# A four-layer graph kernel: the last layer norm is taken out of the head of the last stage and spread over the end of the stage before it

## The chip, the cores and the metric

The kernel runs on one NeuronCore of a Trainium2 chip. Its engines are called here as the profile calls them: PE multiplies matrices (PEld is its weight load, which the profile lists apart), DVE is the vector engine, ACT the scalar engine, POOL the third elementwise engine, and SP issues the transfers from HBM. Each engine works through its own instructions in order, and they wait for each other through semaphores. The metric is the device time of one execution in microseconds (us); lower is better.

## The reference

There are N = 3327 nodes with D = 64 features each, and a dense 0/1 adjacency matrix of 3327 x 3327 (about 0.5% ones). Four layers follow each other. Each one takes a layer norm without weights, a ReLU, a graph layer, and adds the outcome to x:

```python
def _layernorm(x, axis=-1, eps=1e-5):
    m = jnp.mean(x, axis=axis, keepdims=True)
    v = jnp.var(x, axis=axis, keepdims=True)
    return (x - m) / jnp.sqrt(v + eps)
...
    h = jnp.maximum(_layernorm(x, axis=-1), 0.0)
    x = x + _L2_gnn_ref(h, adj, adj, ...)      # layer 2: two GRU cells and an attention term
    h = jnp.maximum(_layernorm(x, axis=-1), 0.0)
    x = x + _L3_gnn_ref(h, adj, r, w_att, b_att)   # layer 3: hyperbolic graph layer
```

Layers 0 and 3 are hyperbolic layers: a sigmoid of pairwise scores, masked by the adjacency and weighted by a function of the pairwise inner products. Layer 1 is a sum with halving weights. Layer 2 is a GRU cell on the sum over neighbours, and a second GRU cell on the mean over neighbours. The change stands where layer 2 ends and layer 3 begins. Layer 3 needs from each row of x its mean, its variance, and the sum of squares of the positive part of the centred row.

## The kernel before

**Layout.** The nodes are padded to 26 tiles of 128 rows (T = 26, P = 128, NP = 3328). `X` holds x in SBUF as 128 partitions x 26 tiles x 64 columns, fp32. Two tiles, t and t + 13, make a pair, so that a turned (transposed) form has 128 rows: 64 features of the one, 64 of the other. `HP` = 1664 is the width of that form. Adjacency masks stay in SBUF as fp8 from layer 1 on.

**Stages.** `hyperbolic_series(None, ...)` is layer 0; it calls `plain_decay` (layer 1), which calls `plain_gat` (layer 2); a second call, `hyperbolic_series(r3, ...)`, is layer 3. A hyperbolic series has a head (layer norm, factors for each node, fp16 parts, turned operands), a long loop over 4 column chunks x 26 row blocks (matmuls at L643/L644, sigmoid L629, mask product L632, arctangent L649, product L654, sums L664/L672), and a tail that puts the result together and stores it.

**The end of layer 2.** In `plain_gat` the columns of the turned form are cut into four groups, `COLS = (0, 4), (4, 3), (7, 3), (10, 3)` (first tile, number of tiles). The eight steps `u` (two GRU cells x four groups) run as a pipeline: products on PE (L1987, L1992), sigmoids (L2000) and tanh (L2011) on ACT, the rest on DVE (L2007, L2008, L2020 to L2027). The result of a group is a sum of up to four fp32 tiles (`oP`, `xh[0][0]`, `hP`, `deg`), still turned. `turn_back(k)` turns it back on PE: for each tile of the group, one matmul for each term of the sum, with the term as the stationary operand and the 128 x 128 identity as the moving one, added up in PSUM (L2043). The last group has one term and uses a transpose (L2041). `scale(k)` then multiplies by the node's diagonal entry `dcol`, on ACT tile by tile (L2059), for the last group on DVE in one go (L2054), and `use(k)` adds to `X` on DVE (L2063).

**Banks and slots.** PSUM is held as four slots of two banks each; `banks` lists them in the order `cnt[0], cnt[1], acc[0], acc[1]`, two entries for each slot, so entries 4 and 5 are one slot, 6 and 7 another. Waits between engines are set by slot, not by bank. The four groups go into entries 4 to 7. `products(u)` uses entries 4 to 7 for even `u` and 0 to 3 for odd `u`.

**The head of layer 3.** All of it is written in one order for all engines (`manual_schedule`), and so is the end of layer 2. On DVE: row means of X in two halves (L449, L450), centring into `H` (L452), variance from squares that ACT makes (L453, L458, L459), an inverse root by bit tricks (L128 to L142, `root_by_bits`), the sum of squares of the positive part (ACT: L455, L456; DVE: L466, L469), then small factors (L471 to L479), the scaled rows `Xr` (L481), the fp16 parts (ACT L482, DVE L484). PE turns those (L542, L517), ACT and DVE copy them out (L524, L522), and the loop begins at L643. POOL fills constant parts of `X0` and `Xe` (L436, L437, L439) and makes a few fp16 columns of each node's factors (L493 to L506), which PE needs from the second half of the turning on. SP fetches the first four `late` tiles for a count that the loop makes (L1447); these reuse memory of layer 2.

**The tail.** When the sums are done, DVE makes the factors `ah`, `am`; ACT multiplies the first 22 tiles of `M` by `am` (L923) while DVE scales `Xr` and adds it and then `M` to X (L916, L919), and X is stored.

Of the kernel before, what the change touches and what calls it, by code (L numbers as in the profile page):

```python
# [10 lines left out]
F32 = mybir.dt.float32  # L11
# [10 lines left out]
P = 128  # L22
# [27 lines left out]
def tile_gnn4(ctx: ExitStack, tc: tile.TileContext, x, adjT, att0, b0, w1, bias1, w_gat, a_gat,  # L50
# [299 lines left out]
    def hyperbolic_series(r, params, ok, masks=None, done=None, ahead=None, then=None, checks=None):  # L350
# [15 lines left out]
        KE = D + 9  # L366
        left_row = rows[0 if r is None else 1]
        W = 512
        with ExitStack() as st:
# [60 lines left out]
            with room(name="hsp", bufs=1) as tp, room(name="hsps", bufs=2, space=PSUM) as ps, \  # L430
                    tc.manual_schedule(engines={mybir.EngineType.Activation, mybir.EngineType.DVE,
                                                mybir.EngineType.PE, mybir.EngineType.Pool}):
                H, R, sq, sr = [tp.tile([P, T, D], F32, name=n) for n in ("H", "R", "sq", "sr")]
# [13 lines left out]
                mean, v, rv, ax, ia2 = [new(n) for n in ("mean", "v", "rv", "ax", "ia2")]  # L447
                for ts in HALVES:
                    V.reduce_sum(mean[:, ts], X[:, ts, :], axis=AX.X)  # L449
                V.tensor_scalar(mean, mean, 1.0 / D, None, op0=OP.mult)  # L450
                for ts in HALVES:
                    V.tensor_sub(H[:, ts, :], X[:, ts, :], wide(mean[:, ts]))  # L452
                    A.activation(sq[:, ts, :], H[:, ts, :], AF.Square)  # L453
                for ts in HALVES:
                    A.activation(R[:, ts, :], H[:, ts, :], AF.Relu)  # L455
                    A.activation(sr[:, ts, :], R[:, ts, :], AF.Square)  # L456
                for ts in HALVES:
                    V.reduce_sum(v[:, ts], sq[:, ts, :], axis=AX.X)  # L458
                V.tensor_scalar(v, v, 1.0 / D, LN_EPS, op0=OP.mult, op1=OP.add)  # L459
                sd, q1, q2 = new("sd"), new("q1"), new("q2")  # L460
                steps = root_by_bits(sd, q1, q2, v)
                next(steps)
                V.reciprocal(rv, v)
                for _ in range(3):
                    next(steps)
                V.reduce_sum(x2[:, HALVES[0]], sr[:, HALVES[0], :], axis=AX.X)  # L466
                for _ in steps:
                    pass
                V.reduce_sum(x2[:, HALVES[1]], sr[:, HALVES[1], :], axis=AX.X)  # L469
                if r is not None:  # L470
                    V.tensor_scalar(rv, rv, cc, None, op0=OP.mult)  # L471
                V.tensor_mul(x2, x2, rv)
# [95 lines left out]
                V.tensor_scalar(right, right, bcol, None, op0=OP.add)  # L568
# [343 lines left out]
            with room(name="hse", bufs=1) as tp:  # L912
# [9 lines left out]
                for t in range(own.start):  # L922
                    A.activation(M[:, t, :], M[:, t, :], AF.Copy, scale=am[:, t:t + 1])  # L923
# [1277 lines left out]
```

## Time and profile before

| what | value |
|---|---|
| median of 3 runs | 721.82 us (719.4 to 724.04) |
| profiled execution, its own time | 719.45 us |
| span of that execution in the profile | 717.7 us |
| busy share PE / DVE / ACT / POOL | 89% / 74% / 76% / 60% |
| end of layer 2 after the last GRU product, 447.4 to 461.3 us | PE busy 9.1 of 13.9 us, DVE 8.5, ACT 6.1 |
| head of layer 3 up to the first `Xr`, 461.3 to 472.7 us | PE idle, DVE busy 10.8 of 11.4 us, ACT 5.2 |
| rest of the head, 472.7 to 488.7 us | PE 13.1 of 16.0 us, DVE 14.1, ACT 10.9, POOL 10.4 |
| loop of layer 3, 488.7 to 693 us | PE busy 203.1 of 204.3 us |

Times inside the execution count from the start of the span. The profile's timeline gives, for each row, start, duration, engine, line, operation, the tile written and the tiles read, and in brackets the idle time before it and whom it waited for; rows of the same kind are merged ("x8"). The chain of waits follows the execution back from its last instruction: each piece is what the next one waited for. Granted clock is the share of full speed that PE had. A matmul in fp32 appears as two records, each with its own weight load.

### The profile page before, as it was taken

How to read it: one execution, taken by the hardware profiler on the slowest of the kernel's cores; microseconds unless marked ns; L12 is line 12 of the kernel's file. 1: busy time of each engine (PE TensorE's matmuls, PEld its weight loads, DVE VectorE, ACT ScalarE, POOL GpSimd, SP SyncE). 2: the span in 40 equal slices, each digit the busy share in tenths (PEclk: the TensorE clock that was granted, in tenths of full speed). 3: DMA queues.
4: the chain of work that ended last, by engine and by line, in shares of the span. 5: the costliest groups of instructions: out<-in, count | busy, mean ns of one | idle time of the engine just before them, and what ended most of it. 6: DMA issues, size and time to landing. Idle time of an engine off the chain costs nothing.

```text
span 717.7 us, 12120 instructions
## 1 busy us (share of the span) xinstructions
PE 636.2 (89%) x4291; PEld 261.4 (36%) x4291; DVE 532.8 (74%) x990; ACT 542.1 (76%) x718; POOL 433.4 (60%) x329
## 2 busy tenths in 40 slices
PE   0799999999999889989998999459999999999970
PEld 0522233333333333435445653443223433333320
DVE  5967778777777799999755428697776877778756
ACT  3688888888888695687881479359888888888853
POOL 2799999989999400205730000039888788887840
PEclk9999999999999999999999999969999999999995
DMA  3998888898878716489960000203325345443001
GB/s 64 313 301 274 259 268 266 277 288 273 268 245 271 258 69 215 137 291 333 402 243 1 2 1 1 95 18 96 89 82 147 105 120 146 116 119 115 25 1 52
DMA packets 61638, 119.25 MB, mean 166 GB/s; under 512 B 9568, under 2 KB 34048, under 8 KB 61568
## 3 DMA queue, kind: packets, MB, share of 16 engines
q1 hardware_dynamic: 57216, 118.38, 51.2%
q10 hardware_dynamic: 4352, 0.02, 0.3%
q8 instruction: 35, 0.57, 0.3%
q14 instruction: 35, 0.29, 0.1%
HBM read 115.64 MB, written 0.88 MB: 162 GB/s over the span
## 4 chain that ended last, share of the span: by engine, by line
PE 67%; DVE 12%; issue 6%; POOL 6%; ACT 4%; DMA 3%; ACTq 1%; POOLq 0%; DVEq 0%
PE slot L664 17%; PE slot L672 9%; PE slot L643 9%; PE slot L1564 9%; PE slot L644 8%; POOL sig L632 6%; PE slot L1578 5%; PE slot L1871 5%; DMA adj<-in 3%; PE slot L1987 2%; PE slot L2043 1%; PE slot L1992 1%; DVE X L1617 1%; ACTq L322 1%; ACT sig L629 1%
## 5 line engine op out<-in xcount | busy, mean ns | idle before, releaser
L654 DVE SCALAR_TENSOR_TENSOR sig<-slot,sig 128x768 f32<-128x768 f32 (+2 forms) x209 | 212.8, 1018 | 105.6 <-POOL sig L632 104.2
L649 ACT ACTIVATE slot<-slot 128x768 f32<-128x768 f32 (+1 forms) x208 | 177.2, 852 | 53.3 <-PE slot L644 53.1
L632 POOL TENSOR_TENSOR sig<-adj,sig 128x768 f32<-128x768 f32 (+2 forms) x105 | 201.7, 1943 | 12.9 <-ACT sig L629 8.4
L629 ACT ACTIVATE sig<-leftB,right 128x768 f32<-128x768 f32 (+2 forms) x210 | 203.5, 970 | 0.5 <-PE pt L517 0.5
L632 POOL TENSOR_TENSOR sig<-mask,sig 128x768 f32<-128x768 fp8e4 (+3 forms) x106 | 173.6, 1651 | 38.2 <-ACT sig L629 37.3
L664 PE MATMUL slot<-sig,Xr 128*64 128x384 f32 (+1 forms) x832 | 169.9, 526 | 3.7 <-DVE sig L654 3.4
L643 PE MATMUL slot<-XC,XT 128*128 128x384 f16 (+1 forms) x416 | 142.2, 342 | 3.1 <-ACT sum L682 1.7
L644 PE MATMUL slot<-XF,XE 73*128 73x384 f16 (+1 forms) x416 | 141.6, 340 | 0.0
L672 PE MATMUL slot<-sig,X 128*32 128x384 f32 (+1 forms) x832 | 94.2, 525 | 0.0
L1570 ACT ACTIVATE w<-slot,ebias 128x832 bf16<-128x832 f32 x76 | 69.0, 951 | 25.3 <-PE slot L1564 24.9
L664 PEld LDWEIGHTS slot<-sig,Xr 128*64 128x64 f32 x832 | 49.8, 135 | 85.7 <-issue 62.7
L643 PEld LDWEIGHTS <-XT 128*128 128x128 f16 x416 | 40.6, 98 | 93.8 <-issue 67.4
L1564 PE MATMUL slot<-mask,rest 128*128 128x416 fp8e4 x208 | 53.9, 341 | 5.0 <-ACT adj L1570 2.8
L1564 PE MATMUL slot<-mask,after 128*128 128x416 fp8e4 x208 | 53.4, 339 | 1.3 <-DVE deg L1588 1.3
L644 PEld LDWEIGHTS <-XE 73*128 73x128 f16 x416 | 40.8, 98 | 28.6 <-issue 4.0
L1459 DVE TENSOR_SCALAR_CACHE_REDUCE same<-late 128x832 fp8e4<-128x832 f32 x48 | 48.4, 1009 | 0.0
L219 POOL TENSOR_TENSOR mask<-mask,offdiag 128x128 fp8e4<-128x128 fp8e4 x26 | 17.5, 684 | 44.4 <-PE slot L1564 44.3
L436 POOL MEMSET X<- 128x832 f32 x2 | 1.6, 791 | 69.6 <-ACT xh L1978 69.6
L1871 PE MATMUL slot<-mask,own 128*64 128x384 fp8e4 (+1 forms) x416 | 39.6, 345 | 2.6 <-DVE deg L1588 2.6
L672 PEld LDWEIGHTS slot<-sig,X 128*32 128x32 f32 x832 | 16.4, 108 | 67.7 <-issue 67.7
L542 PE MATMUL pt<-ident_h,Xp 128*64 128x128 f16 x32 | 2.6, 314 | 37.7 <-ACT Xp L482 37.7
L1578 PE MATMUL slot<-w,h 128*64 128x416 bf16 x304 | 34.0, 345 | 0.0
(341 smaller groups left out, 696.2 us busy)
## 6 DMA issues: line engine op xcount, KB each, us to landing
adj<-in SPq DMA_DIRECT2D x78, 384.0 KB, 5.2
late<-in SPq DMA_DIRECT2D x48, 416.0 KB, 3.2
adj<-in SPq DMA_DIRECT2D x17, 832.0 KB, 7.2
adj<-in SPq DMA_DIRECT2D x27, 512.0 KB, 5.8
ahead<-in SPq DMA_DIRECT2D x14, 832.0 KB, 7.7
ahead<-in SPq DMA_DIRECT2D x16, 416.0 KB, 5.7
own<-in SPq DMA_DIRECT2D x16, 416.0 KB, 5.8
own<-in SPq DMA_DIRECT2D x8, 832.0 KB, 10.1
```

Of the source, the lines that this page charges most:

```text
L629: A.activation(sig[:, os], leftB[c][:, os], AF.Sigmoid, bias=right[:, b:b + 1])
L632: G.tensor_tensor(sig[:, os], adj[:, os], sig[:, os], op=OP.mult)
L643: PE.matmul(L[:, o, :c[1] * P], XT[:, rows], XC[c][:, o, :], start=True, stop=False)
L644: PE.matmul(L[:, o, :c[1] * P], XE[:KE, rows], XF[c][:, o, :], start=False, stop=True)
L649: A.activation(L, L, AF.Arctan, scale=PA / SX ** 2)
L654: V.scalar_tensor_tensor(sig[:, os], slot[:, os, :tiles[k][0][1] * P], PC, sig[:, os], op0=OP.add, op1=OP.mult)
L664: PE.matmul(acc[c][o * D:(o + 1) * D, 0, :n], Xr[:, b, :], sigs[k][:, o, :], start=b == 0, stop=b == T - 1)
L672: PE.matmul(acc[c][q:q + 32, 1, :n], X0[:, b - 1 + i, :], w[:, o, :], start=b == 1, stop=b == T - 1, tile_position=(0, q))
L1564: PE.matmul(cnt[o][:, h, :BK], w, cols(k, o, h), start=w is after and steps[k][1] == T - 1, stop=True, skip_group_check=True)
L1570: A.activation(ws[k][:, o, :, :], cnt[o][:, :, :BK], AF.Exp, scale=-LN2, bias=ebias)
L1578: PE.matmul(acc[c][o * D:(o + 1) * D, h, :BK], parts[i][:, b, :], w[:, o, h, :], start=b == T - 1 and i == 0, stop=b == 0 and i == 1)
L1871: PE.matmul(acc[k][o * D:(o + 1) * D, :], w, mask[:, of(k, o * HP)], start=n == 0 and i == 0, stop=n == T - 1 and i == 1)
```

## The change

The second layer norm is prepared inside layer 2.

- In block 12 of layer 2's loop, `centre()` takes the row means of X (kept in `ln.mean`) and subtracts them from X in place.
- Every tile of the GRU result is turned back with `centring` (identity minus the mean over each half of 64) in place of the identity, so that what is added to X has mean zero and X stays centred. The last group becomes a matmul like the others.
- The mean of what was added is needed too, since x itself needs it at the end. `turn_means()` repeats all products with a 128 x 2 moving operand `means` into PSUM entry 7. `new_means()` adds the result to `ln.mean`.
- The four groups go to entries 4, 6, 0 and 2, one in each slot.
- Group 1 is scaled and added on DVE, tile by tile (`use_at_once`), not by ACT and DVE.
- Squares, positive parts, their squares and the row sums are made group by group behind each addition, in tiles of the GRU that are free by then (`xh`). Variance, root, `x2` and the reciprocal are finished there.
- Layer 3 takes `H = X`, and its own means, centring, squares and sums are left out. The mean comes back as the bias of an ACT instruction: for 22 tiles in the tail, for the last 4 in the head.

```diff
                                                 mybir.EngineType.PE, mybir.EngineType.Pool}):
-                H, R, sq, sr = [tp.tile([P, T, D], F32, name=n) for n in ("H", "R", "sq", "sr")]
+                H = R = sq = sr = None
+                if ln is None:
+                    H, R, sq, sr = [tp.tile([P, T, D], F32, name=n) for n in ("H", "R", "sq", "sr")]
                 Xe = tp.tile([P, T, KE + 9], F16, name="Xe")
                 E, Fe = Xe[:, :, D:KE], Xe[:, :, KE:]
                 G.memset(X0, 0.0)
...
-                mean, v, rv, ax, ia2 = [new(n) for n in ("mean", "v", "rv", "ax", "ia2")]
...
+                ax, ia2, q1, q2 = [new(n) for n in ("ax", "ia2", "q1", "q2")]
+                x2s = x2 if ln is None else ln.x2
+                if ln is None:
...
+                else:
+                    H, rv, sd = X, ln.rv, ln.sd
                 if r is not None:
                     V.tensor_scalar(rv, rv, cc, None, op0=OP.mult)
-                V.tensor_mul(x2, x2, rv)
+                V.tensor_mul(x2, x2s, rv)
                 V.tensor_scalar(ax, x2, 1.0, None, op0=OP.subtract)
                 V.reciprocal(ia, ax)
                 V.tensor_scalar(root, x2, 1.0, None, op0=OP.max)
...
                     copy_on(on, XF[c][:, o, :], turned16(lambda t: Xp[:, t, D:], KE, *range(t, t + c[1])))
                 V.tensor_mul(right, lr[:, :, 1], z)
                 V.tensor_scalar(right, right, bcol, None, op0=OP.add)
+                if ln is not None:
+                    for t in range(own.start, own.stop):
+                        A.activation(X[:, t, :], X[:, t, :], AF.Identity, bias=ln.mean[:, t:t + 1])
                 V.scalar_tensor_tensor(root, root, ROOT, zs, op0=OP.mult, op1=OP.mult)
                 V.tensor_scalar(small["k"], ia, 0.5 * PF, None, op0=OP.mult)
                 V.tensor_scalar(small["bx"], ax, -1.0, None, op0=OP.mult)
...
                 def added(a, ts):
                     V.tensor_add(X[:, ts, :], X[:, ts, :], a[:, ts, :])
 
-                own = slice(T - 4, T)
                 for t in range(own.start):
-                    A.activation(M[:, t, :], M[:, t, :], AF.Copy, scale=am[:, t:t + 1])
+                    A.activation(M[:, t, :], M[:, t, :], AF.Identity, scale=am[:, t:t + 1], bias=ln.mean[:, t:t + 1])
                 for ts in HALVES:
                     scaled(Xr, ah, ts)
                     added(Xr, ts)
...
             xh = [[pers.tile([P, HP], F32, name=f"xh{g}{o}") for o in range(2)] for g in range(2)]
             oP = H.rearrange("p k o d -> p (k o d)")
             wgT = pers.tile([D, D], F32, name="wgT")
+            centring = pers.tile([P, P], F32, name="centring")
+            means = pers.tile([P, 2], F32, name="means")
+            G.memset(means, 0.0)
+            for o in range(2):
+                G.memset(means[o * D:(o + 1) * D, o:o + 1], 1.0 / D)
+            V.tensor_sub(centring.rearrange("p (o d) -> p o d", o=2), ident.rearrange("p (o d) -> p o d", o=2),
+                         wide(means))
             hundred = pers.tile([P, 1], F32, name="hundred")
             V.memset(hundred, -100.0)
             for _ in range(1):
...
                     V.scalar_tensor_tensor(deg, deg, -1.0, r0, op0=OP.mult, op1=OP.mult)
                     V.scalar_tensor_tensor(deg, deg, 2.0, r0, op0=OP.add, op1=OP.mult)
 
-                todo = {3: lambda: degrees(2, 4), 4: lambda: degrees(3, 6), 12: lambda: (weights2(4), inverse()),
+                def centre():
+
+                    V.reduce_sum(ln.mean, X, axis=AX.X)
+                    V.tensor_scalar(ln.mean, ln.mean, 1.0 / D, None, op0=OP.mult)
+                    V.tensor_sub(X, X, wide(ln.mean))
+
+                todo = {3: lambda: degrees(2, 4), 4: lambda: degrees(3, 6), 12: lambda: (weights2(4), inverse(), centre()),
                         13: lambda: turn(0, 6), 15: lambda: weights3(5), 17: inverse2, 19: lambda: turn(4, 7),
                         20: lambda: turn(8, 4), 23: lambda: turn(12, 6)}
                 V.tensor_scalar(zo[:, 2 * T:2 * T + 2], zo[:, 2 * T:2 * T + 2], first, None, op0=OP.mult)
...
                 d2 = dcol.rearrange("p (h t) -> p h t", h=2)
                 turned, scaled = {}, {}
 
+                BACK = 4, 6, 0, 2
+
+                def terms_of(k):
+                    return [oP] if k == C - 1 else [oP, hP, deg] if k > 1 else [oP, xh[0][0], hP, deg]
+
                 def turn_back(k):
 
-                    terms = [oP] if k == C - 1 else [oP, hP, deg] if k > 1 else [oP, xh[0][0], hP, deg]
                     t0, n = COLS[k]
-                    pt = turned[k] = bank(4 + k)
+                    pt = turned[k] = bank(BACK[k])
                     for t in range(n):
-                        cs = slice((t0 + t) * P, (t0 + t + 1) * P)
-                        for i, src in enumerate(terms):
-                            if len(terms) == 1:
-                                PE.transpose(pt[:, t * P:(t + 1) * P], src[:, cs], ident)
-                            else:
-                                PE.matmul(pt[:, t * P:(t + 1) * P], src[:, cs], ident, start=i == 0,
-                                          stop=i == len(terms) - 1)
+                        product(pt[:, t * P:(t + 1) * P], k, t0 + t, centring)
+
+                def product(to, k, t, w):
+                    terms = terms_of(k)
+                    for i, src in enumerate(terms):
+                        PE.matmul(to, src[:, t * P:(t + 1) * P], w, start=i == 0, stop=i == len(terms) - 1)
+
+                def turn_means():
+                    pt = turned["means"] = bank(7)[:, :2 * C2]
+                    for k in range(C):
+                        for t in range(COLS[k][0], COLS[k][0] + COLS[k][1]):
+                            product(pt[:, 2 * t:2 * t + 2], k, t, means)
+
+                def new_means():
+                    t = tp.tile([P, 2, C2], F32, name="dm")
+                    V.tensor_mul(t, turned["means"].rearrange("p (t h) -> p h t", h=2), d2)
+                    V.tensor_add(halves(ln.mean), halves(ln.mean), t)
+
+                def halves(t):
+                    return t.rearrange("p (h t) -> p h t", h=2)
 
                 def of_bank(k):
                     n = COLS[k][1]
...
                 def use(k):
                     t0, n = COLS[k]
                     V.tensor_add(X2[:, :, t0:t0 + n, :], X2[:, :, t0:t0 + n, :], scaled[k][:, :, :n, :])
+
+                def use_at_once(k):
+                    t0, n = COLS[k]
+                    for h in range(2):
+                        for t in range(n):
+                            to = X2[:, h, t0 + t, :]
+                            V.scalar_tensor_tensor(to, of_bank(k)[:, h, t, :], d2[:, h, t0 + t:t0 + t + 1], to,
+                                                   op0=OP.mult, op1=OP.add)
+
+                sq, pos, sr = xh[1][0], xh[1][1], xh[0][1]
+
+                def group(t, k):
+                    t0, n = COLS[k]
+                    return t.rearrange("p (h t d) -> p h t d", h=2, d=D)[:, :, t0:t0 + n, :]
+
+                def squares(k):
+                    t0, n = COLS[k]
+                    A.activation(group(sq, k), X2[:, :, t0:t0 + n, :], AF.Square)
+
+                def positive(k):
+                    t0, n = COLS[k]
+                    A.activation(group(pos, k), X2[:, :, t0:t0 + n, :], AF.Relu)
+
+                def squares_of_positive(k):
+                    A.activation(group(sr, k), group(pos, k), AF.Square)
+
+                def variance(k):
+                    t0, n = COLS[k]
+                    V.reduce_sum(halves(ln.v)[:, :, t0:t0 + n], group(sq, k), axis=AX.X)
+
+                def norms2(t0, n):
+                    V.reduce_sum(halves(ln.x2)[:, :, t0:t0 + n],
+                                 sr.rearrange("p (h t d) -> p h t d", h=2, d=D)[:, :, t0:t0 + n, :], axis=AX.X)
 
                 for k in (2, 3):
                     mean(k)
...
                 tanh(K - 1)
                 scale(0)
                 turn_back(1)
-                scale(1)
                 turn_back(2)
                 state(K - 1)
+                turn_back(3)
+                turn_means()
                 use(0)
-                turn_back(3)
-                use(1)
+                squares(0)
+                positive(0)
+                use_at_once(1)
+                squares(1)
+                variance(0)
+                variance(1)
                 scale(2)
                 scale(3)
+                use(3)
+                squares(3)
                 use(2)
-                use(3)
+                squares(2)
+                for k in (0, 1, 3, 2):
+                    if k:
+                        positive(k)
+                    squares_of_positive(k)
+                variance(3)
+                variance(2)
+                V.tensor_scalar(ln.v, ln.v, 1.0 / D, LN_EPS, op0=OP.mult, op1=OP.add)
+                steps = root_by_bits(ln.sd, *ln.qs, ln.v)
+                next(steps)
+                V.reciprocal(ln.rv, ln.v)
+                for _ in range(3):
+                    next(steps)
+                norms2(0, COLS[2][0])
+                for _ in steps:
+                    pass
+                norms2(COLS[2][0], C2 - COLS[2][0])
+                new_means()
 
     def load():
         for ts in HALVES:
...
     wt, bias, wg, gru = middle_weights()
     zo = const.tile([P, 2 * T + 2 + EARLY + len(LATE)], F32, name="zo")
     first = const.tile([P, 1], F32, name="first")
+    ln = SimpleNamespace(mean=const.tile([P, T], F32, name="mean2"), qs=[bias[:, i * T:(i + 1) * T] for i in range(2)],
+                         **{n: wt[:, i * T:(i + 1) * T] for i, n in enumerate(("v", "x2", "rv", "sd"))})
     V.memset(first, 0.0)
     for o in (0, D):
         V.memset(first[o:o + 1, :], 1.0)
```

`V` is DVE, `A` ACT, `G` POOL. The hunks left out pass `ln` along as an argument.

## Prediction

> **What bounds the kernel now.** I read the page first, then the chain of waits, then the timeline and the groups of instructions around 447 to 489 us. By stages the change can only act between the last GRU product (447.4 us) and the loop of layer 3 (488.7 us). Before it nothing on the path moves, and behind it the loop keeps PE busy for 203.1 of 204.3 us, so a shift of its start is a shift of the end. The chain there, with start and duration in us:
>
> ```profile
> 447.49 3.78 PE slot L2043 x32
> 451.30 1.75 ACT x L2059 x8
> ...
> 453.10 4.96 PE slot L2043 x42
> 458.05 0.34 PE slot L2041 x3
> ...
> 458.42 1.34 ACT x L2059 x6
> ...
> 460.34 0.95 DVE X L2063 x2
> ...
> 465.49 1.97 DVE v L458 x2
> ...
> 472.72 1.98 DVE Xr L481 x2
> ```
>
> PE turns four groups, the end of that is added to X by 461.29, and 11.4 us of layer norm on DVE follow until `Xr` starts at 472.72. The second group waits, since its bank lies in the slot that ACT still reads:
>
> ```profile
> 451.30 1.74 ACT L2059 ACTIVATE x<-slot,dcol 128x64 f32<-128x64 f32 x8 [0.41 <-PE slot L2043]
> 453.10 0.49 PE L2043 MATMUL slot<-ident,own 128*128 128x128 f32 x2 [1.83 <-ACT x L2059]
> ```
>
> **What the change removes.** With one slot for each group that wait goes. Records of L2043 follow each other every 0.1115 us (42 of them, with 0.1 to open, from 453.10 to the next line's first at 457.89). So 32 + 42 records from 447.42, and 6 for the last group, which is now three products of two records, end at 456.4 instead of 458.4: 2.0 us. The data are there: the last state (L2027) ends at 453.42, before PE reaches its group at 455.7. The means (L449, L450: 2.2 us) and the centring (L452: 2.0, half of it under ACT's squares) go from the head. In block 12 they cost 2.0 + 0.2 + 1.9 us on DVE between 401.0 and 410.8, where DVE waits 9.7 us for ACT's L1937. Without that cover it would be 4.1 us.
>
> **What it adds: `turn_means`.** The four groups have 4 x 4 + 3 x 4 + 3 x 3 + 3 x 1 = 40 products, repeated with two moving columns. The stationary operand is still a whole 128 x 128 fp32 tile, loaded anew for each of two records: 80 weight loads. Nothing in the trace has just this form, so its price is bounded from rows.
>
> ```profile
> L664 PEld LDWEIGHTS slot<-sig,Xr 128*64 128x64 f32 x832 | 49.8, 135 | 85.7 <-issue 62.7 <-DVE sig L654 22.6 <-DVE same L1459 0.2
> L672 PEld LDWEIGHTS slot<-sig,X 128*32 128x32 f32 x832 | 16.4, 108 | 67.7 <-issue 67.7
> L2043 PEld LDWEIGHTS slot<-ident,deg 128*128 128x128 f32 x20 | 3.0, 192 | 0.0
> ```
>
> The mean of one fp32 load goes 108, 135, 192 ns for 32, 64, 128 columns: 0.87 ns a column over a fixed 80 ns, so 0.11 us of streaming for 128. The starts say the same. Two loads that open a burst overlap only in the fixed part:
>
> ```profile
> 447.42 0.30 PEld L2043 LDWEIGHTS slot<-ident,own 128*128 128x128 f32 x2 [0.60 <-ACT gate L2000]
> 478.90 1.24 PEld L560 LDWEIGHTS <-XT 128*128 128x128 f16 x26
> ```
>
> 0.30 less 0.19 is a start every 0.11 us for fp32. The fp16 loads of L560, with six moving columns, come about every 0.03 us ((1.24 - 0.10) / 25 is 0.046 with one pause in it), and that at half clock. [...] by the rows above 80 x 0.108 = 8.7 us. [...] I take 8.7 us at full clock. [...] Above: 80 x 0.192 = 15.4 with nothing overlapped.
>
> Who waits: entry 7 lies in the slot of entry 6, where group 1 is. `turn_means()` is written ahead of `use_at_once(1)`, so that DVE instruction waits for the last mean product, not for group 1 (ready at 453.7). Queued behind it on DVE are both first variance sums, `scale(3)` and `use(3)`, `use(2)`; on ACT `squares(1)` waits for it, with `scale(2)` and all later squares behind. So the norm's work starts over at T, the end of `turn_means`: 456.4 + 8.7 = 465.1 at full clock. Only `use(0)`, `squares(0)`, `positive(0)` lie under it.
>
> **The clock.** [...] The window rows list stretch, length, busy time of PE, PEld, DVE, ACT and POOL with counts, granted clock, DMA:
>
> ```profile
> 381.04:384.45 3.41, 1.53 (x15) 1.08 (x15) 1.79 (x4) 0.00 (x0) 0.00 (x0) 1.00 0.02 5
> 384.45:387.86 3.41, 3.41 (x19) 2.15 (x20) 1.28 (x2) 0.00 (x0) 0.00 (x0) 0.50 0.00 0
> 459.55:462.96 3.41, 0.00 (x0) 0.00 (x0) 3.14 (x5) 0.20 (x1) 0.00 (x0) 1.00 0.97 370
> 462.96:474.70 11.74, 0.00 (x0) 0.00 (x0) 11.14 (x27) 6.06 (x7) 2.50 (x5) 0.50 0.07 28
> ```
>
> A stretch of 3.41 us with PE 45% busy was enough to halve the clock for the next one, and so was one with no matmul. In `turn_means` PE has weight loads without a gap, but two moving columns per 0.108 us. [...] whether loads alone count as busy, no row here shows. If they don't, the drop falls at the end of the first stretch that is less than half dense: between 458.1 and 461.5, about 459.8. Then 31 of 80 records are done and 49 follow at 2 x 0.107: T = 470.4 (468.7 to 472.2). If they count, T stays 465.1.
>
> **From T to `Xr`.** DVE: six tiles at the 0.196 us spacing of L1617's 128 x 64 form plus latency, 1.3. ACT then: squares(1) 0.5 and scale(2) 1.3, to T + 3.2. DVE meanwhile: sums of groups 0 and 1 (0.6 + 0.5), scale(3) 0.5, use(3) 0.6, then use(2), to T + 4.0. ACT: squares(2) 0.5, then 0.6 and three times 1.0 for the positive parts and their squares, to T + 8.1. DVE: last norm sum 0.95, then x2, ax, reciprocal, two factors as at L472 to L479, 1.4: `Xr` at T + 10.4. (ACT durations from L453's 0.89 for 832 columns and L2000's 0.87 ns a column.) That is one us shorter than the 11.4 behind 461.29; splitting into groups takes back most of what left the path. The DVE chain of root steps lies under ACT here.
>
> Small ones. POOL's fill of `X0` and `Xe` (0.8 + 0.7) now waits for the last norm sum, since those tiles reuse what it reads. The fp16 columns then are ready 7.2 us after `Xr` starts, not 6.0; PE asks for them at 7.35: 0 to 0.5, I take 0. The `late` fetches wait for mean products, so they start near T instead of 457.9, the fourth at T + 9; the first of them is counted at 489.6 + shift, and chunk operands queued behind on SP (479.2) are later too: 0. Four ACT additions of the mean (0.9) fit in ACT's 1.8 us wait before `leftB`. The tail's ACT has a bias more at 0.244 spacing: 0 to 0.3, I take 0. PE stays idle past the next stretches either way, so the head's start at half clock (until 480.02) remains. None of these can fall below nothing: they only move or add work.
>
> **Sum and rivals.** `Xr` starts at T + 10.4 against 472.72.
> - *Clock drops under the mean products*, chance 0.66: 470.4 + 10.4 - 472.7 = +8.1 us (+6.4 to +9.9). On the profile's own 719.45 that is 727.6; on the median of 721.82, which lies 2.4 higher, 729.9. For it: the 45% row. Against it: gapless loads.
> - *Clock holds*, 0.26: +2.8, 724.6. Slower still, within what can be told.
> - *Mean products are cheap* (not slower), 0.08: loads at L560's pace end at 458.5 to 458.7, so T + 10.4 = 469.1, -3.7 us, 718.1. It decides below 0.071 us a record, where T is 462.3. Against it stand the 0.11 us starts of every fp32 burst. The change then would do what it says: group work under PE.
>
> A measurement of this kernel tells about 1%, 7.2 us, from no change. Of the first case about three quarters lie beyond it. Hence slower 0.50, within 0.48, faster 0.02. The range 723.3 to 732.3 holds the first two cases with the spread of medians (1.5) on the first's late drop; it leaves out the third and the tails. The first case's own is 727.5 to 732.3.
>
> **What would show it.** In the profile after: group records without the 1.8 us wait, ending near 456.4; 80 mean records with starts 0.108 apart, then 0.21 once the clock reads 0.50; the first DVE `X<-slot` tile waiting for PE, not before 465; `Xr` 10.4 us behind the last mean product; loop and tail as long as before. Starts of 0.03 us, or a wait that ends with group 1 near 453.7, would prove me wrong.

## The result and the profile after

The changed kernel takes 731.8 us (median of 4 runs, 731.47 to 733.88) against 721.62 us for the kernel before (median of 4 runs, 719.4 to 724.04). The ratio is 1.0146, with a 95% interval of 1.0109 to 1.0184: slower by 10.2 us. The profiled execution has a span of 729.6 us, 11.9 us more than the profile of before. 1.6 us of that are there when the turning of the groups begins. They are older than the changed parts of layer 2: the first product of layer 0's loop is 1.2 us later (32.07 against 30.91), the first of layer 2's loop 1.7 us (381.80 against 380.14). In all the kernels below the first record of the turned groups lies between 446.4 and 449.7 us, in one of them at 446.85 although nothing ahead of the groups differs from the kernel before. So I count from that record (447.42 us before, 449.04 us after); counted so, the two profiles are 10.3 us apart.

These timeline rows of the changed kernel answer to the rows of the groups shown of before:

```profile
449.04 0.49 PE L2069 MATMUL slot<-centring,own 128*128 128x128 f32 x2
...
457.40 0.83 PE L2069 MATMUL slot<-centring,own 128*128 128x128 f32 x6
458.07 0.28 PE L2069 MATMUL slot<-means,own 128*128 128x2 f32 x2
...
468.76 1.42 PE L2069 MATMUL slot<-means,own 128*128 128x2 f32 x6
470.22 1.05 DVE L2109 SCALAR_TENSOR_TENSOR X<-slot,dcol,X 128x64 f32<-128x64 f32 x5 [14.57 <-PE slot L2069]
```

The groups run without a gap and are through 9.2 us after their first record; before it took 11.0. Then come the 80 mean records, and the first tile of `use_at_once(1)` waits on DVE for 14.57 us until the last of them is done. Its group's last record had ended at 455.56, and DVE has been idle since 455.65.

The windows of the same stretch (length, busy us of PE, PEld, DVE, ACT and POOL with counts, granted clock, DMA share, GB/s) show the clock:

```profile
449.04:458.07 9.03, 9.03 (x84) 9.03 (x81) 6.40 (x13) 4.55 (x13) 0.00 (x0) 1.00 0.01 2
458.07:463.52 5.45, 5.45 (x52) 5.45 (x50) 0.00 (x0) 0.00 (x0) 0.00 (x0) 1.00 0.00 0
463.52:470.22 6.70, 6.66 (x32) 6.57 (x31) 0.00 (x1) 0.00 (x0) 0.00 (x0) 0.50 0.12 16
```

In the first 5.45 us of the mean products 49 of the 80 records go by, 0.1115 us from one start to the next. Then the clock is halved, with PE and its weight loads busy throughout, and the last 31 take 6.7 us, about 0.215 each. DVE and ACT do next to nothing in either row.

Behind that wait, three rows of the timeline are longer than I had them. The end of the norm:

```profile
479.32 0.80 POOL L439 MEMSET X<- 128x832 f32 x1 [97.61 <-DVE dm L2079]
479.37 1.27 DVE L480 TENSOR_SCALAR ax<-x 128x26 f32<-128x26 f32 x1
480.05 0.23 POOL L440 MEMSET Xe<- 128x78 f16 x1
480.15 0.46 POOL L442 MEMSET Xe<- 128x26 f16 x3
481.52 1.97 DVE L488 SCALAR_TENSOR_TENSOR Xr<-X,ia 128x832 f32<-128x832 f32 x2
```

The same step in the kernel before:

```profile
471.59 0.18 DVE L473 TENSOR_SCALAR ax<-x 128x26 f32<-128x26 f32 x1
```

The first sigmoid of layer 3, with PE's last transposes of `Xe` ahead of it, and the sigmoid and its product on POOL in the kernel before:

```profile
492.80 0.94 PE L524 MATMUL pt<-ident_h,Xe 128*82 128x128 f16 x10 [0.19 <-DVE XE L529]
493.82 2.37 ACT L639 ACTIVATE sig<-leftB,right 128x512 f32<-128x512 f32 x3 [1.47 <-DVE XE L529]
494.62 2.16 POOL L642 TENSOR_TENSOR sig<-mask,sig 128x512 f32<-128x512 fp8e4 x2 [6.26 <-ACT sig L639]
```
```profile
483.45 1.32 ACT L629 ACTIVATE sig<-leftB,right 128x512 f32<-128x512 f32 x2
484.24 2.16 POOL L632 TENSOR_TENSOR sig<-mask,sig 128x512 f32<-128x512 fp8e4 x2 [4.76 <-ACT sig L629]
```

Before, the sigmoid ran as soon as ACT had made `leftB`; now it is 1.47 us behind that. The row names DVE's copy as what ended the wait, but the sigmoid starts 0.08 us behind the end of PE's last transposes (493.74).

And the scaling of `M` at the end, here and in the kernel before:

```profile
715.59 7.40 ACT L932 ACTIVATE M<-M,mean,am 128x64 f32<-128x64 f32 x22 [5.20 <-DVE am L870]
722.37 1.22 DVE L929 TENSOR_TENSOR X<-X,M 128x448 f32<-128x448 f32 x2 [1.29 <-ACT M L932]
```
```profile
705.36 5.36 ACT L923 ACTIVATE M<-M,am 128x64 f32<-128x64 f32 x22 [5.20 <-DVE am L860]
709.34 2.03 DVE L919 TENSOR_TENSOR X<-X,M 128x832 f32<-128x832 f32 x3
```

With that, the 10.3 us have their places. "Tile" is the start of the first `use_at_once(1)` tile on DVE; all values are in us. The first two columns count from the first group record, the next three are lengths: from `Xr` to the first product on POOL, from there to the scaling of `M`, from there to the end of the span. The last is the span's end, from the first group record.

| kernel | tile | Xr | to POOL | loop | tail | end |
|---|---|---|---|---|---|---|
| before | - | 25.3 | 11.5 | 221.1 | 12.3 | 270.3 |
| after | 21.2 | 32.5 | 13.1 | 221.0 | 14.0 | 280.6 |
| difference | | +7.2 | +1.6 | -0.1 | +1.7 | +10.3 |

### The profile page after: what moved, and what is told of

Same layout as the page of the kernel before. It is cut to its first block, busy times and chain, and to the rows that moved or that the text cites. A ratio compares the mean times of both kernels' runs of the same rounds, so it can differ in the third digit from the quotient of the medians.

```text
span 729.6 us, 12298 instructions
## 1 busy us (share of the span) xinstructions
PE 649.5 (89%) x4374; PEld 275.4 (38%) x4374; DVE 535.8 (73%) x998; ACT 544.6 (75%) x722; POOL 431.4 (59%) x332
## 5 line engine op out<-in xcount | busy, mean ns | idle before, releaser
L642 POOL TENSOR_TENSOR sig<-adj,sig 128x768 f32<-128x768 f32 (+2 forms) x105 | 201.7, 1947 | 14.5 <-ACT sig L639 11.0
L219 POOL TENSOR_TENSOR mask<-mask,offdiag 128x128 fp8e4<-128x128 fp8e4 x26 | 15.3, 598 | 46.8 <-PE slot L1573 46.8
```

The source lines that it names most:

```text
L642: G.tensor_tensor(sig[:, os], adj[:, os], sig[:, os], op=OP.mult)
```

## The experiments

My theory after the prediction and these rows: the mean products cost their weight loads, stretched by a halved clock, and all of it counts because one DVE instruction waits for them; three smaller costs stand behind it. The rival was that the norm by groups is long in itself. Each ratio below is to the kernel before in runs taken together with the experiment's (medians 720.85 to 721.13 us), and the experiments start from the changed kernel, but for the last.

**Without the means.**

```diff
                 turn_back(3)
-                turn_means()
...
-                new_means()
```

> The changed kernel without turn_means and new_means. Left out: the mean of what the GRU adds is not added to the mean of X. Times here are counted from the first record of the group products (before: Xr at +25.3 us; after the change: first X<-slot tile at +21.2, Xr at +32.5). Theory 1, the 80 mean records on PE stand ahead of the first X<-slot tile and of everything behind it: that tile starts at about +5.0 to +6.6, when group 1 is turned and the first use is done, and Xr at +16.5 to +18, so 15 us earlier than with the change. With the tail's +2.0 and the first sigmoid's +1.4 still there the kernel is 4 to 5 us faster than before. Rival, the norm by groups is long in itself and the mean products only fill time in which ACT and DVE would have worked anyway: Xr comes 5 us earlier at most (+27 or later), and the kernel stays slower than before by 5 us.

Measured: 0.9932 (0.9911 to 0.9953) of before, 4.9 us faster. The timeline of this kernel:

```profile
452.95 1.24 DVE L2109 SCALAR_TENSOR_TENSOR X<-slot,dcol,X 128x64 f32<-128x64 f32 x6
...
464.66 1.97 DVE L488 SCALAR_TENSOR_TENSOR Xr<-X,ia 128x832 f32<-128x832 f32 x2
```

From the first group record at 446.39 that is +6.6 for the tile and +18.3 for `Xr`, 14.2 us earlier than with the means; `Xr` is 0.3 past the range that I had given. The rival falls. The tile no longer waits, and the norm behind it is about as long as with the means (11.7 us against 11.3).

**The means in another slot.**

```diff
-                    pt = turned["means"] = bank(7)[:, :2 * C2]
+                    pt = turned["means"] = bank(5)[:, :2 * C2]
```

> The changed kernel with the means in entry 5 instead of 7, that is, in the slot of group 0, whose reader is done, and not in that of group 1. The same 80 records. Theory 1, the wait of the first X<-slot tile is for the slot and not for PE's time as such: the tile starts at +5 to +6.6 from the first group record instead of +21.2, the norm runs beside the mean products, and what still waits for their end is new_means, the last DVE step before Xr. Xr then is 1.4 to 2.5 us behind the last mean record (+21.1): +22.5 to +23.6, against +25.3 before and +32.5 with the change. The whole is within 1.5 us of before, with the tail and the first sigmoid still later. Rival, PE's time is what counts, whoever waits: Xr stays near +32.5 and the kernel 10 us slower than before.

Measured: 1.0025 (1.0009 to 1.0041), 1.8 us slower than before, 723.02 us in the median against 731.8 with the change. Its timeline:

```profile
455.17 1.05 DVE L2109 SCALAR_TENSOR_TENSOR X<-slot,dcol,X 128x64 f32<-128x64 f32 x5
...
464.67 0.80 POOL L439 MEMSET X<- 128x832 f32 x1 [83.39 <-DVE wt L2134]
...
470.24 0.18 DVE L2079 TENSOR_TENSOR dm<-slot,dcol 128x26 f32<-128x26 f32 x1 [5.78 <-PE slot L2069]
...
470.56 0.17 DVE L480 TENSOR_SCALAR ax<-x 128x26 f32<-128x26 f32 x1
...
471.62 1.97 DVE L488 SCALAR_TENSOR_TENSOR Xr<-X,ia 128x832 f32<-128x832 f32 x2
```

The total is 0.3 us over what I expected, with an interval of 0.6 to 3.0 us. The same 80 records, ending no earlier than with the change (+21.6 against +21.2), but the tile goes at +6.6 and `Xr` at +23.0. The slot was the wait; one digit moves it from the first step of the norm to the last, `new_means`, which sits 5.78 us idle. The fill of `X0` falls into that idle time, and `ax` takes 0.17 us.

**The mean products with 128 moving columns.**

```diff
-            means = pers.tile([P, 2], F32, name="means")
+            means = pers.tile([P, P], F32, name="means")
...
-                            product(pt[:, 2 * t:2 * t + 2], k, t, means)
+                            product(pt[:, 2 * t:2 * t + P], k, t, means)
```

> The changed kernel with 128 moving columns in each mean product (the two of the means and 126 of zeros, which later products overwrite) instead of two. The same 80 weight loads. Theory 1, a record costs its load, and the clock fell because only two columns moved: records stay 0.1115 us apart to the end, the clock reads 1.00 under all of them, and the last ends at +18.0 from the first group record instead of +21.1; Xr at +29.3, the kernel 3 us less slow than with the change (+7 us on before). Rival A, the clock falls at that point for another reason: 0.50 from +14.5 again and an end at +21 or later. Rival B, the moving columns cost too: records over 0.15 apart at full clock and an end beyond +21.

Measured: 1.0097 (1.0058 to 1.0135), 7.0 us slower than before. The windows of the mean products (columns as above), and the tile:

```profile
457.75:463.50 5.75, 5.75 (x54) 5.75 (x53) 0.00 (x0) 0.00 (x0) 0.00 (x0) 1.00 0.00 0
463.50:466.89 3.39, 3.35 (x31) 3.16 (x29) 0.00 (x0) 0.00 (x0) 0.00 (x0) 1.00 0.00 0
```
```profile
466.89 1.24 DVE L2110 SCALAR_TENSOR_TENSOR X<-slot,dcol,X 128x64 f32<-128x64 f32 x6 [11.54 <-PE slot L2069]
```

Sixty-four times as many moving columns, and the products end 3.0 us sooner (+18.2 against +21.2). So the columns don't set the price: a record takes 0.1115 us at full clock with 2 or with 128 of them, and the weight loads are busy in 5.75 of the first 5.75 us. And the clock read 1.00 through all 80 records, 9.1 us, where the only difference is the columns that move; how many are needed was not tried.

**The means in the same product as the tile.** If a record takes 0.1115 us with 2 or with 128 columns and two more are next to free, the means can be columns 129 and 130 of the centring matrix.

```diff
-            centring = pers.tile([P, P], F32, name="centring")
-            means = pers.tile([P, 2], F32, name="means")
+            both = pers.tile([P, P + 2], F32, name="both")
+            centring, means = both[:, :P], both[:, P:]
...
-                        product(pt[:, t * P:(t + 1) * P], k, t0 + t, centring)
+                        product(last if t == 3 else pt[:, t * BOTH:(t + 1) * BOTH], k, t0 + t, both)
```

`BOTH` is 130. Four such tiles, 520 columns, don't fit into the 512 of an entry, so the fourth tile of group 0, `last`, lies in entry 5.

> The changed kernel with the two mean columns as columns 129 and 130 of the centring matrix, so that one weight load gives the centred tile and its means; turn_means is gone, the fourth tile of group 0 goes to entry 5, and the means are taken from the banks of the groups in five small DVE products, ahead of the last norm sum. Theory 1, the loads are the cost and two more moving columns are free: group records stay about 0.112 apart and end at +9.0 from the first, the first X<-slot tile starts at +5 to +6.6, Xr at +17 to +18.5, and the kernel is 3.5 to 5 us faster than before with the tail and the first sigmoid still later. Rival, what the means cost comes back on DVE or in the group products: Xr at +20 or later.

Measured: 0.9939 (0.9919 to 0.9959), 4.4 us faster than before. The timeline:

```profile
457.24 0.83 PE L2070 MATMUL slot<-both,own 128*128 128x130 f32 x6
...
467.70 1.03 DVE L488 SCALAR_TENSOR_TENSOR Xr<-X,ia 128x832 f32<-128x832 f32 x1
```

The group records end where they ended without the means (+9.2 from 448.87), and `Xr` is at +18.8. That is 0.3 above the upper end of what I expected: `new_means` is five small products and one sum on DVE now; together they take 0.6 us, and DVE has no gap there.

The next three undo the smaller costs one at a time, with the mean products as they are in the change. None can be told by its total: with T, the end of the mean products, between +21.2 and +21.8, and the head's clock (below), one such kernel differs from the next by up to 2 us. Their rows decide.

**The mean added in the loop.** The four additions in the head of layer 3 go too; the cut leaves that hunk out.

```diff
+                if ln is not None and 2 <= j < 2 + T:
+                    t = j - 2
+                    A.activation(X[:, t, :], X[:, t, :], AF.Identity, bias=ln.mean[:, t:t + 1])
...
-                    A.activation(M[:, t, :], M[:, t, :], AF.Identity, scale=am[:, t:t + 1], bias=ln.mean[:, t:t + 1])
+                    A.activation(M[:, t, :], M[:, t, :], AF.Copy, scale=am[:, t:t + 1])
```

> The changed kernel with the mean added to X in the loop of layer 3 (one tile a step on ACT, from the third step on) instead of in the last scaling of M, which is the plain copy with a scale again. Theory 1, in the changed kernel that scaling is 2.0 us longer (7.40 us for 22 tiles against 5.36 before) because each takes a second column, and the last sums of X wait for it: 5.4 us again, the time from the start of the scaling to the end of the profile 2.0 us shorter than the 14.0 us of the changed kernel, the loop as long as it was; in all 2 us less than with the change. Rival, the additions (26 of 0.2 to 0.3 us) delay the loop's ACT work: the loop is longer by 2 to 6 us and nothing is won.

Measured: 1.0144 (1.0123 to 1.0166), no gain in the total. From its timeline and its groups (busy us, mean ns, idle):

```profile
717.09 5.36 ACT L932 ACTIVATE M<-M,am 128x64 f32<-128x64 f32 x22 [5.20 <-DVE am L867]
```
```profile
L912 ACT ACTIVATE X<-X,mean 128x64 f32<-128x64 f32 x26 | 8.8, 337 | 0.0
```

The scaling takes 5.36 us again, 0.244 a tile and not 0.336, and the tail is 12.5 us and not 14.0. So the bias, with `Identity` in place of `Copy`, is the cost of the scaling. The loop gives 0.6 back (221.5 us); the rest of the missing gain lies ahead of the loop, in 14.4 us from `Xr` to POOL instead of 13.1, and in T, 0.5 later. T lies ahead of the edit. On the way from `Xr` to POOL the edit only removes ACT's four additions; the clock returned late there (eight `pe` products take 1.80 us and not 1.06), as it did in three kernels that keep them (below).

**The old layout.**

```diff
-                H = R = sq = sr = None
-                if ln is None:
-                    H, R, sq, sr = [tp.tile([P, T, D], F32, name=n) for n in ("H", "R", "sq", "sr")]
+                H, R, sq, sr = [tp.tile([P, T, D], F32, name=n) for n in ("H", "R", "sq", "sr")]
```

> The changed kernel with the four tiles of the old norm (H, R, sq, sr) allocated again for layer 3, though nothing uses them: Xe and all tiles behind it lie where they lay before the change. Theory 1, the first sigmoid of layer 3 waits in the changed kernel for the last transposes of Xe, since its tile lies on Xe: now it follows leftB, its idle time ahead is at most 0.3 us instead of 1.47, and from Xr to the first product on POOL it is 11.5 us (before: 11.5) instead of 13.1; 1.4 us less in all. Rival, the sigmoid would wait anyway, for PE or POOL: still 13 us from Xr to the first product on POOL.

Measured: 1.0134 (1.0114 to 1.0153). Its timeline:

```profile
493.04 1.32 ACT L637 ACTIVATE sig<-leftB,right 128x512 f32<-128x512 f32 x2
493.83 2.17 POOL L640 TENSOR_TENSOR sig<-mask,sig 128x512 f32<-128x512 fp8e4 x2 [4.53 <-ACT sig L637]
```

From `Xr` to POOL it is 11.4 us, and the profile from the first group record is 279.2 us, 1.4 less than after the change. The sigmoid now starts ahead of PE's last transposes of `Xe`, which end at 494.52 here. So the wait came with the layout. That leaving out the four tiles had moved `Xe` to where the sigmoid's tile lies is argued from the order in which the tiles are placed.

**Scratch exchanged.**

```diff
-                sq, pos, sr = xh[1][0], xh[1][1], xh[0][1]
+                sq, pos, sr = xh[0][1], xh[1][1], xh[1][0]
```

> The changed kernel with two scratch tiles exchanged: the squares of the positive parts, which the last norm sum reads, no longer lie where X0 will be; the squares for the variance do, and they are read some 2 us earlier. Theory 1, the subtraction ax took 1.27 us in the changed kernel (0.17 to 0.19 elsewhere) because POOL filled X0 and Xe at that very time: the fill now starts by 1.5 us or more ahead of it, ax takes 0.2 us, and Xr is 10.2 to 10.4 us behind the end of the mean products instead of 11.3. Rival, ax is slow for another reason (its operand, its place behind the sum): still 1.2 us or more with the fill elsewhere.

Measured: 1.016 (1.0118 to 1.0202). Its timeline:

```profile
475.01 0.80 POOL L439 MEMSET X<- 128x832 f32 x1 [94.22 <-DVE wt L2183]
475.05 1.28 DVE L128 TENSOR_SCALAR wt<-wt 128x26 int32<-128x26 int32 x1
475.74 0.23 POOL L440 MEMSET Xe<- 128x78 f16 x1
475.84 0.46 POOL L442 MEMSET Xe<- 128x26 f16 x3
...
479.88 0.18 DVE L480 TENSOR_SCALAR ax<-x 128x26 f32<-128x26 f32 x1
```

A miss that says more than a hit. The fill starts 4.9 us ahead of `ax` now, `ax` is at 0.18 us, and the 1.1 us now stand on the root step that met the fill. `Xr` is 11.2 us behind T, as with the change. The cost belongs to the meeting, not to `ax`.

**All four together.**

The edits of merged, tail_copy, layout and scratch in one kernel; there is no other.

> The mean columns in the centring matrix, the mean added in the loop, the old layout and the exchanged scratch tiles together. If the four costs add: Xr at +17.5 to +18 us from the first group record (+18.8 with the merged columns alone, +25.3 before), and from Xr to the end as before (245 us instead of 248): 7 to 8 us faster than before, a ratio of 0.989 to 0.991. Rival, one of the four only covers another (a head at half clock that ends later, or a loop that is slower by the additions): 4 to 5 us faster than before, as with the merged columns alone (0.994).

Measured: 0.9876 (0.9852 to 0.9900) of before: 8.9 us by the ratio, 8.3 us by the medians, more than I expected. Its profile, of the slowest of its four runs, shows 6.2 us from the first group record on; where the rest lies I have no row for. `Xr` is at +18.7 and not at the expected +17.5 to +18, since `scratch` is one of the four and gives nothing. From `Xr` to the end it is 245.4 us, as before (245.0).

**The fill early.** As all four, but nothing is left on the tile that becomes `X0`:

```diff
-                sq, pos, sr = xh[1][0], xh[1][1], xh[0][1]
+                sq, pos = xh[1]
...
-                    A.activation(group(sr, k), group(pos, k), AF.Square)
+                    A.activation(group(pos, k), group(pos, k), AF.Square)
```

> As all_four, but the squares of the positive parts are written over the positive parts themselves, so that the tile on which X0 will lie is free after the GRU. Theory 1, the first DVE step with a number as operand that meets POOL's fill waits for the end of the whole fill (ax 1.27 us with the change; a root step 1.28 us in scratch and in all_four): with X0 filled near 440 us and Xe near 458 us, where DVE does no such step, both take 0.18 us, Xr is at +17.6 us from the first group record (all_four: +18.7), and the kernel is 9 to 10 us faster than before (ratio 0.986 to 0.988). Rival, the 1.1 us goes to another step again, since DVE is busy without a gap there: Xr at +18.5 or later, the ratio of all_four (0.9876).

Measured: 0.9905 (0.9873 to 0.9938), 712.78 us, which in time can't be told from all four (712.86). The 9 to 10 us that I expected are not shown by it: the ratio gives 6.8 us, with an interval of 4.5 to 9.2. The timeline can tell the two kernels apart:

```profile
439.08 0.80 POOL L437 MEMSET X<- 128x832 f32 x1 [57.98 <-ACT xh L1998]
...
460.68 0.18 DVE L128 TENSOR_SCALAR wt<-wt 128x26 int32<-128x26 int32 x1
...
465.11 0.18 DVE L478 TENSOR_SCALAR ax<-x 128x26 f32<-128x26 f32 x1
...
466.17 1.03 DVE L486 SCALAR_TENSOR_TENSOR Xr<-X,ia 128x832 f32<-128x832 f32 x1
```

Both steps take 0.18 us, and `Xr` is at +17.7 from 448.43, the 1.0 us that the exchange had not brought.

**The kernel before with four slots alone.**

```diff
-                    pt = turned[k] = bank(4 + k)
+                    pt = turned[k] = bank((4, 6, 0, 2)[k])
```

> The kernel before with one edit: its four turned groups in entries 4, 6, 0 and 2, so each in a slot of its own. Theory 1, the removed wait is worth what the prediction put it at: group products without a gap, X complete 2.0 us earlier, Xr at +23.3 us from the first group record (before: +25.3), and the kernel 2 us faster (ratio 0.997). Rival, ACT's scaling of the last groups and DVE's sums are the later ones, so that PE's wait only moves to them: Xr at +24.5 or later, less than 1 us.

Measured: 0.9974 (0.9959 to 0.9988), 1.9 us faster. `Xr` is at +22.4 from 446.85: in the profile the removed wait is worth 2.9 us at `Xr`, not 2.0 (in time the interval is 0.9 to 3.0). Its groups' last scaling, then the same step in the kernel before:

```profile
455.41 1.34 ACT L2059 ACTIVATE x<-slot,dcol 128x64 f32<-128x64 f32 x6 [0.68 <-PE slot L2043]
```
```profile
458.42 1.33 ACT L2059 ACTIVATE x<-slot,dcol 128x64 f32<-128x64 f32 x6 [1.00 <-PE slot L2041]
```

Groups 2 and 3 shared a slot too. So ACT's scaling of group 2 waited for the products of group 3 (L2041), and now it waits for its own (L2043).

The same table for all the runs:

| kernel | tile | Xr | to POOL | loop | tail | end |
|---|---|---|---|---|---|---|
| no_means | 6.6 | 18.3 | 13.1 | 221.0 | 14.1 | 266.4 |
| other_slot | 6.6 | 23.0 | 14.3 | 221.0 | 14.3 | 272.6 |
| wide_means | 18.2 | 29.5 | 14.6 | 221.0 | 14.0 | 279.1 |
| merged | 6.6 | 18.8 | 13.1 | 221.0 | 14.1 | 266.9 |
| tail_copy | 21.7 | 33.0 | 14.4 | 221.5 | 12.5 | 281.5 |
| layout | 21.4 | 32.7 | 11.4 | 221.1 | 13.9 | 279.2 |
| scratch | 21.8 | 33.0 | 14.4 | 221.0 | 13.9 | 282.3 |
| all_four | 6.6 | 18.7 | 11.5 | 221.7 | 12.1 | 264.1 |
| fill_early | 6.6 | 17.7 | 11.5 | 221.8 | 12.1 | 263.1 |
| four_slots | - | 22.4 | 11.5 | 221.1 | 12.3 | 267.4 |

## Why the prediction was right, and where it was not

The forecast of 729.9 us, in a range up to 732.3, was 1.9 us short. Its likeliest case happened, by the mechanism it named. But that closeness is partly luck: one term came out 1.8 us smaller, and three that I had set to nothing added 4.2 us. And it was near an even bet, 0.50 for slower against 0.48 for a difference too small to tell.

- **The groups** end at +9.2, 1.8 us earlier on PE, where 2.0 was worked out. What this wait was worth on the path was under-read: four_slots shows 2.9, since a second pair of groups shared a slot. I looked at PE's wait alone and not at ACT's 1.00 us wait in the same rows.
- **Centring in block 12** costs nothing that shows: the changed kernel is 1.7 us behind at the first product of layer 2's loop, ahead of that block, and 1.6 us behind at the groups.
- **80 weight loads** at 0.108 us: 0.1115 measured at full clock, 0.215 at half. The 0.03 us case is out, by this run and by wide_means. Two sums were off without effect: 80 x 0.108 is 8.6, not 8.7, and the cheap case decides below 5.9 / 80 = 0.074 us a record, not 0.071.
- **Who waits**: right, and other_slot and no_means show it. Without that wait the same products cost 9.5 us less at `Xr`, without the products at all 14.2.
- **The clock** fell under the mean products, as the case with chance 0.66 said, but at +14.5 and not at +12.4. So 49 records ran at full clock and not 31, and T was 1.8 us earlier than I had it (+21.2 against +23.0), just outside my range for it. That step was mis-sized. I placed the fall at the end of the first stretch of 3.41 us that is less than half dense. That was an estimate from the kernel before: behind a stretch with PE 45% busy the clock read 0.50, behind one with 57% (449.30 to 452.72, PE 1.96 of 3.42 us) it read 1.00. Counted back from the fall by this length, the stretch from 456.69 to 460.11 was one: group records fill its first 1.4 us, 40%. The clock stayed. It fell one stretch later, at the end of the first that held mean records alone. In other_slot it fell at such a place too, 14.0 us behind the first group record, by the granted clock of 0.92 from 458.0 to 463.5 and 0.50 behind; for tail_copy, layout and scratch it would be at +14.2 to +14.6, an estimate from their T and records of 0.1115 and 0.215 us. wide_means shows that the few moving columns are the reason: with 128 the clock read 1.00 to the end.
- **From T to `Xr`**, "10.4 us": 11.3, of which 1.1 are `ax`'s wait. The step that failed is "POOL's fill of `X0` and `Xe` ... 0 to 0.5, I take 0". I asked who needs what POOL writes late, not which DVE step would meet the fill.
- **"Loop and tail as long as before"** failed twice. From `Xr` to POOL it is 1.6 us longer: I had the four dropped tiles as work saved, and never asked what then lies on their place. layout shows it. And "The tail's ACT has a bias more ... 0 to 0.3, I take 0" was 2.0 us of ACT, 1.7 at the end: 0.092 us more for each of 22 tiles (tail_copy).

In sum: +8.1 predicted for `Xr`, less 1.8 for T, plus 0.9 behind T, is the +7.2 measured. With 1.6 for the sigmoid, 1.7 for the tail and -0.1 for the loop it is +10.3 in the profile (before rounding the terms), +10.2 in the medians.

What stays open: the 1.1 us of the fill, the 1.6 of the sigmoid and the 1.7 of the tail are each read from the rows of one profile, of the run that takes it away. By total time tail_copy, layout and scratch can't be told from the change, nor fill_early from all_four.

## What to carry to other kernels

Price a small fp32 product with a full 128 x 128 stationary operand by its weight load, not by its columns: here a second pass over the same operands cost as much for each record as the first, 0.1115 us, and 0.215 once the clock fell, while two more moving columns in the first pass cost nothing that shows (its records end at +9.2 with and without them). When a change frees or drops a tile, ask what now lies on that memory and who will wait for its last reader (1.6 us here); and when it moves a fill to POOL's late end, ask which DVE step will meet it (1.1 us here). A gain that an engine makes early counts only if no instruction ahead in the other engine's queue waits on a shared slot (9.5 us at `Xr` in other_slot).

## What the runs showed of the hardware

- **A DVE `TENSOR_SCALAR` that met POOL's fill waited for the end of the whole fill.** `ax` took 1.27 us in the changed kernel, no_means, wide_means, merged, tail_copy and layout, and a root step 1.28 us in scratch and all_four. Each ended 0.02 to 0.03 us behind the last of five memsets in a row (0.80, 0.23 and 0.46 us for the last three); without a meeting these steps took 0.17 to 0.18. Other DVE operations were not held up: in the kernel before a `SCALAR_TENSOR_TENSOR` that started at 438.59, during the fill of `X0` (437.99 to 438.78), took its usual 0.62 us, and in four_slots a `TENSOR_TENSOR` at 455.74, during the fill of `Xe`, its usual 0.56. The step stopped for five instructions and not for the one it met. The cause was not shown: the runs show only that the delay follows the fill.
- **Weight loads without a gap did not keep TensorE's clock**: with two moving columns it fell to 0.50 after 5.45 us, with 128 it stayed at 1.00 through all 80 records. In the kernel before PE is idle from 458.38, and there the clock fell at 462.96, 4.58 us later. From the start of the mean records to the fall is 0.9 us more than from the start of the idle time: in these two profiles the loads kept the clock little longer than an idle PE did.
- **The half-clock stretch differs in length, and the way from `Xr` to POOL goes with its end.** It lasted 17.07 us before (462.96 to 480.02) and 23.89 after (463.52 to 487.41), 5 and 7 times the 3.41 us of the stretch at 0.50 from 384.45 to 387.86 in the kernel before. In other_slot, wide_means, tail_copy and scratch the half clock still shows in PE's eight `pe` products (L583 in tail_copy, L586 in the others), which take 1.75, 1.91, 1.80 and 1.78 us, and the way from `Xr` to POOL took 14.3 to 14.6 us; in the changed kernel and no_means the same eight take 1.06 us, and the same way took 13.1. In the changed kernel the full clock came back 5.9 us behind `Xr`. So 1.2 to 1.5 us of a total go with when the clock returns. No edit here set that, so that the late clock is the cause is argued.
- **ACT's scaling of 22 tiles of 128 x 64** took 7.40 us, 0.336 a tile, as `Identity` with a second column (the changed kernel), and 5.36 us, 0.244 a tile, as `Copy` without it (tail_copy and the kernel before).
